# Two steps between norms or ternary weights and their transposes, and sums copied out of PSUM, in a four-layer network

## The chip, the core and the metric

The kernel runs on one core of one Trainium2 chip. The number that counts is the device time of one execution in microseconds (us). A core has four engines that compute and run side by side, each strictly in the order of its own queue: TensorE (PE in the profile; its weight loads, which overlap its matmuls, are PEld), VectorE (DVE), ScalarE (ACT) and GpSimd (POOL). They work on two memories on the chip, SBUF and PSUM; PE writes to PSUM alone. Three executions of the kernel before took 1842.01, 1845.6 and 1845.91 us, a median of 1845.6.

## The reference, cut to what matters

Four layers, each a cross-attention and then a feed-forward network, each added to `x` (2048 tokens of 256 numbers). The context has 1601 rows. The change lies in the feed-forward parts of the second and third layer (L1 and L2) and in what prepares their weights; the attention between them and after them is touched in passing.

```python
x = x + L0_xattn(layernorm(x), ctx)
x = x + L0_ffn(layernorm(x))
x = x + L1_xattn(layernorm(x), ctx, mask)
x = x + L1_ffn(layernorm(x))
x = x + L2_xattn(layernorm(x), ctx)
x = x + L2_ffn(layernorm(x))
x = x + L3_xattn(layernorm(x), ctx, mask)
x = x + L3_ffn(layernorm(x))

def L1_ffn(x):                      # 256 -> 1024 -> 256, rank 16 beside it
    h = bitlinear(x, w_fc) + gate * (x @ v.T @ fast_b.T @ u.T)
    r = maximum(h, 0)
    return bitlinear(r * r, w_proj) # weights rounded to -1, 0, 1 times a row's scale

def L2_ffn(x):                      # 256 -> 1024 -> 256
    h = gelu(ternary_linear(x, w_up))
    return ternary_linear(h, w_down)

def ternary_linear(x, w):           # weights -1, 0, 1 about half their mean size
    w_t = sign(w) * (abs(w) > 0.5 * mean(abs(w)))
    rms = sqrt(sum(x * x, -1)) / sqrt(x.shape[-1])
    return (x / (rms + 1e-8)) @ w_t.T
```

So the second `ternary_linear` of layer L2 divides each token's output by the root mean square of its 1024 hidden values, which is known only when all of them are.

## The kernel before, in words

**Tiles.** A partition is one of 128 rows (`P`). The tokens go in 4 chunks (`NCH`) of 512 (`CH`), each of 4 tiles of 128 tokens (`TPC`). `self.x` keeps all 16 tiles of the residual stream in SBUF. PSUM is shared out in three kinds of tiles: `psc`, 3 tiles of two banks each, for all products that are soon read; and one bank each of `pa` and `pm`, mostly for sums that stay for a while.

**Stages.** After layer 0's attention, `fast_layers` (L2503) runs seven stages: e0 (layer 0's feed-forward, to about 915 us of the profile), a1 (attention of layer 1, to 985), f1 (its feed-forward, to 1130), a2 (to 1335), f2 (to 1475), a3 (to 1735) and f3. Each stage is a loop of steps ("turns"). The order of PE is the order of the program, by hand: what the program issues first, PE does first. The orders of DVE, ACT and POOL are set when the kernel is built, close to the program's order.

**Work in the background.** While a stage's loop runs, two kinds of generators are advanced beside it. One prepares the weights of the next stage; it is opened and queued after 3/16 of the loop's turns. The other kind, `norm_into` (L1272), makes the normalized and transposed input of one chunk; `ahead(c)` at the start of chunk c completes the norm of chunk c and puts that of chunk c+1 at the front. After each turn `side` (L1258) advances the generator at the front by so many steps as the stage's rate says (2 in a1, f1, a2, f2), and a step ends at a `yield`. At the end of a loop `ready` runs what is left of the next stage's weights, and of its first norm, at once:

```python
def side(self, n=1):
    while n and self.bg:
        if next(self.bg[0], self) is self:
            self.bg.popleft()
        else:
            n -= 1

def finish(self, gen):
    while gen in self.bg:
        self.side()
    drain(gen)
```

`finish` advances by one step at a time. Where the norm at the front turns out to be at its end, `side` takes it away and runs one step of the generator behind it, the next weights.

**A norm.** `norm_into` has, for a chunk: statistics of the 4 tiles on DVE (two steps, L1278, L1279), the inverse root on POOL (one step, L1283 to L1293; in f2 with a root mean square too), four `xn` tiles on DVE (two steps, L1298), and then 8 transposes on PE into one `psc` tile (L1307) with copies out of it (one step): six steps. In f1 and f2 (`split`) the copies are `xh` on ACT (L1314, a cast to the format that PE takes at its full speed) and `xl` on DVE (L1315, what that cast left), alternating for two halves, each waiting for the one before.

**Feed-forward of layers 1 and 2, `fast_ffn` (f1 and f2).** A chunk has four turns. Turn n issues `up(n)`: 8 matmuls of 128x512 over `xh` and `xl` (L1708; in f1 two more, L1713, with `z`, a small product that `low_rank` makes at each chunk's start from `xh` and `xl`, L1691 to L1697); then `down(n - 2)`: 16 matmuls of 128x256 (L1749), which add to `accs`, the one `pa` and the one `pm` bank. Between them ACT, DVE and POOL turn the product into `hi` and `lo`: in f2 a gelu and a cast on ACT (L1718, L1719), `lo` and the square `sq` on DVE (L1720, L1722), and the sum of squares on POOL (L1728, L1730); in f1 ACT does L1734 and L1736, DVE the square L1735, POOL `lo` (L1737). So `down` of a chunk's last groups is issued after the first two `up` of the next chunk. `close(c)` follows the last `down` of a chunk: in f2 it sums the squares over the hidden values with matmuls by a column of ones (L1762), copies the four sums (L1767), makes the inverse root on POOL and DVE (`rms_inverse`, L157 to L160), and adds the four tiles to `x` (L1771) straight from the banks `pa` and `pm`. The next chunk's first `down` needs these banks again, and there is one of each.

**Ternary weights.** `ternary_transposed` (called by the weights generators of f1 and f2) makes the -1, 0, 1 tile `t` on DVE in six steps and then, in two steps, transposes it on PE (L1540) into a `psc` tile that ACT copies (L1541). In f1's weights, L1606 and L1616 belong to the small product that follows. L1350 to L1389 are in the weights of the attention a2, prepared during f1; L2120 is in those of a3, prepared during f2.

**Attention of layer 3, `fast3`.** Scores of a head group go through an exponential on ACT into `p` tiles (L2230), of which five are there; two are made for each group of 128 keys (L2223) and read by `values`. `verdict`, at the end of layer 0's attention, decides from the masks which branch is run; its tile `some` lies in the pool `small`.

Of the kernel before, what the change touches and what calls it, by code (L numbers as in the profile page):

```python
# [9 lines left out]
F32 = mybir.dt.float32  # L10
F32R = mybir.dt.float32r
BF16 = mybir.dt.bfloat16
AF = mybir.ActivationFunctionType
ALU = mybir.AluOpType
# [36 lines left out]
class Net:  # L51
# [1217 lines left out]
            self.side()  # L1269
        drain(gen)  # L1270

    def norm_into(self, pool, c, made, split=False, rms=False, bufs=2):  # L1272

        nc = self.nc
        st = self.small.tile([P, TPC, 6], F32, name="st")
        mv = self.small.tile([P, TPC, 2], F32, name="mv")
        for i in range(TPC):
            nc.vector.bn_stats(st[:, i, :], self.x[c * TPC + i])  # L1278
            nc.vector.bn_aggr(mv[:, i, :], st[:, i, :])  # L1279
            if i % 2:  # L1280
                yield
        rstd = self.small.tile([P, TPC], F32, name="rstd")
        nc.gpsimd.tensor_scalar_add(rstd, mv[:, :, 1], LN_EPS)  # L1283
        nc.gpsimd.tensor_tensor(rstd, rstd, self.mhalf, ALU.pow)
        if rms:

            r = self.small.tile([P, TPC], F32, name="rms")
            nc.gpsimd.tensor_tensor(r, mv[:, :, 1], self.phalf, ALU.pow)
            nc.gpsimd.tensor_tensor(r, r, rstd, ALU.mult)
            nc.gpsimd.tensor_scalar(r, r, 1e-8, None, ALU.add)  # L1290
            ri = self.small.tile([P, TPC], F32, name="rmsi")
            nc.vector.reciprocal(ri, r)
            nc.gpsimd.tensor_tensor(rstd, rstd, ri, ALU.mult)  # L1293
        yield
        xns = []
        for i in range(TPC):
            xn = pool.tile([P, D], F32, name="xn", bufs=4)
            nc.vector.tensor_scalar(  # L1298
                xn, self.x[c * TPC + i], mv[:, i, 0:1], rstd[:, i : i + 1], ALU.subtract, ALU.mult
            )  # L1300
            xns.append(xn)
            if i % 2:
                yield
        ps = self.psc()
        for kc in range(2):
            for i in range(TPC):
                nc.tensor.transpose(  # L1307
                    ps[:, kc, i * P : (i + 1) * P], xns[i][:, kc * P : (kc + 1) * P], self.ident
                )
        if split:  # L1310
            xh = pool.tile([P, 2, CH], F32R, name="xh", bufs=2)
            xl = pool.tile([P, 2, CH], F32R, name="xl", bufs=2)
            for kc in range(2):
                nc.scalar.copy(xh[:, kc, :], ps[:, kc, :])  # L1314
                nc.vector.tensor_tensor(xl[:, kc, :], ps[:, kc, :], xh[:, kc, :].bitcast(F32), ALU.subtract)  # L1315
            made[c] = xh, xl
        else:
            xnT = pool.tile([P, 2, CH], F32, name="xnT", bufs=bufs)
            nc.scalar.copy(xnT[:, 0, :], ps[:, 0, :])  # L1319
            nc.vector.tensor_copy(xnT[:, 1, :], ps[:, 1, :])  # L1320
            made[c] = xnT
        yield
# [199 lines left out]
    def ternary_transposed(self, rawp, w, half, nhalf, place):  # L1522


        nc = self.nc
        n, m = w.shape[1:]
        lo = rawp.tile([P, n, m], BF16, name="lo")
        t = rawp.tile([P, n, m], BF16, name="t")
        for h in range(2):
            ns, shape = slice(h * n // 2, (h + 1) * n // 2), [P, n // 2, m]  # L1530
            nc.vector.tensor_tensor(lo[:, ns, :], w[:, ns, :], nhalf[:, ns, :].to_broadcast(shape), ALU.is_lt)
            yield
            nc.vector.tensor_tensor(t[:, ns, :], w[:, ns, :], half[:, ns, :].to_broadcast(shape), ALU.is_gt)
            yield
            nc.vector.tensor_tensor(t[:, ns, :], t[:, ns, :], lo[:, ns, :], ALU.subtract)
            yield
        for out, blocks in place:
            ps = self.psc(BF16, 1024)
            for k, (o, i) in enumerate(blocks):
                nc.tensor.transpose(ps[:, 0, k * P : (k + 1) * P], t[:, o, i * P : (i + 1) * P], self.identb)  # L1540
            nc.scalar.copy(out, ps[:, 0, :])  # L1541
            yield
# [134 lines left out]
    def fast_ffn(self, st, tail):  # L1677
# [79 lines left out]
        def close(c):  # L1757
            if gelu:
                ps = self.psc()
                for i in range(TPC):  # L1760
                    for j in range(2):
                        nc.tensor.matmul(  # L1762
                            ps[:, 0, i : i + 1], lhsT=sqs[c][:, j, i * P : (i + 1) * P], rhs=self.ones[:, 0:1],
                            start=j == 0, stop=j == 1,
                        )
                ss = self.small.tile([P, TPC], F32, name="ss2")
                nc.vector.tensor_copy(ss, ps[:, 0, :TPC])  # L1767
                ri = self.rms_inverse(ss, NF * P)
                for i in range(TPC):
                    x = self.x[c * TPC + i]  # L1770
                    nc.vector.scalar_tensor_tensor(  # L1771
                        x, accs[c][i // 2][:, (i % 2) * D : (i % 2 + 1) * D], ri[:, i : i + 1], x, ALU.mult, ALU.add
                    )
            else:
                for b in range(2):
                    y = pool.tile([P, 2, D], F32, name="y")
                    nc.vector.tensor_tensor(
                        y, accs[c][b].rearrange("p (i d) -> p i d", i=2),
                        w["out"].unsqueeze(1).to_broadcast([P, 2, D]), ALU.mult,
                    )  # L1780
                    x = self.xc[c][:, 2 * b : 2 * b + 2, :]
                    nc.gpsimd.tensor_tensor(x, x, y, ALU.add)
# [388 lines left out]
    def fast3(self, st, tail):  # L2171
# [46 lines left out]
        def scores(u, kt):  # L2218
            g, q = u % G, queries[u][0]
            pair = [self.psc() for _ in range(2)]  # L2220
            for j in range(4):
                hs = slice(32 * j, 32 * j + 32)
                nc.tensor.matmul(  # L2223
                    pair[j // 2][:, j % 2, :], lhsT=w["kT"][hs, g, kt * P : (kt + 1) * P], rhs=q[hs, :],
                    start=True, stop=True,
                )
            weights[u, kt] = []
            for k in range(2):
                p = pool.tile([P, 2, CH], F32, name="p", bufs=5)
                nc.scalar.activation(p, pair[k], AF.Exp, scale=DH**-0.5)  # L2230
                weights[u, kt].append(p)

# [237 lines left out]
    def verdict(self):  # L2470

        nc = self.nc
        some = self.small.tile([P, KEPT], BF16, name="some", bufs=1)
        sums = self.const.tile([P, 4], F32, name="sums")
        said = self.const.tile([P, 1], mybir.dt.int32, name="said")
        nc.vector.tensor_reduce(sums[:, 0:1], self.fl, AX.XYZ, ALU.add)
        ps = self.pm()
        nc.tensor.matmul(ps[:, 0:1], lhsT=self.ones, rhs=sums[:, 0:1], start=True, stop=True)
        nc.vector.tensor_scalar(sums[:, 1:2], ps[:, 0:1], 0.0, None, ALU.is_equal)
        nc.vector.tensor_scalar(some, self.row0[0], 0.0, None, ALU.not_equal)  # L2480
        nc.vector.tensor_reduce(sums[:, 2:3], some, AX.X, ALU.max)
        nc.vector.tensor_tensor(sums[:, 3:4], sums[:, 1:2], sums[:, 2:3], ALU.mult)
        nc.vector.tensor_copy(said, sums[:, 3:4])
        return said
# [70 lines left out]
    def layers(self):  # L2555
        def weights1(w, r):
            away = w.tile([P, KEPT], F32, name="away1")
            self.nc.vector.tensor_scalar(away, self.row0[0], 0.0, NEG, ALU.is_equal, ALU.mult)
            return self.fast1_weights(w, r, "L1_xattn", NCTX - KEPT, KEPT, away=away)

        def weights2(w, r):
            return self.fast1_weights(w, r, "L2_xattn", 0, NCTX, biases=True)

        split = {"split": True}
        self.fast_layers([
            ("e0", "left", self.fast0_weights, {"bufs": NCH}, self.fast0, 64, 1, 15),
            ("a1", "right", weights1, {}, self.fast1, 16, 2),
            ("f1", "left", self.fast_ffn1_weights, split, self.fast_ffn, 16, 2),
            ("a2", "right", weights2, {}, self.fast1, 16, 2),
            ("f2", "left", self.fast_ffn2_weights, {"rms": True, **split}, self.fast_ffn, 16, 2),  # L2570
            ("a3", "right", self.fast3_weights, {}, self.fast3, 48, 1),
            ("f3", "left", self.fast_ffn3_weights, {}, self.fast_ffn3, 16, 2),
        ])
# [109 lines left out]
```

## Time and profile before

| what | value |
|---|---|
| runs of the kernel | 1842.01, 1845.6, 1845.91 us, median 1845.6 |
| the profiled execution | 1846.99 us |
| its span, first to last instruction | 1844.9 us |
| mean granted clock of TensorE | 0.956 of full |
| f1's transposes L1307 for chunks 1, 2, 3 start at | 1008.40, 1029.53, 1062.20 us |
| f2's sums L1762 start at | 1377.30, 1407.56, 1438.32, 1469.86 us |
| f2's transposes L1307 for chunks 1, 2, 3 start at | 1363.84, 1391.21, 1420.10 us |

The profile is of one execution. Its span is 2.1 us shorter than the time of that execution, and this execution was 1.4 us longer than the median. Times within it are in us from the first instruction. A line such as `PE pa L1749 <- DVE x L1771` says that matmuls of line 1749 into the tile `pa` stood waiting until instructions of line 1771 on DVE, which write `x`, were done. In a timeline a line gives the start, the duration, the engine, the source line, the operation, the tiles (out<-in), shapes, how many instructions are put together, and in brackets the idle time of the engine ahead of it with what ended that. In a table of stretches each engine has its busy time and its number of instructions, and PEclk is the clock that TensorE was granted, as a part of full speed; matmuls take longer when it is below 1.

### The profile page before, as it was taken

How to read it: one execution, taken by the hardware profiler on the slowest of the kernel's cores; microseconds unless marked ns; L12 is line 12 of the kernel's file. 1: busy time of each engine (PE TensorE's matmuls, PEld its weight loads, DVE VectorE, ACT ScalarE, POOL GpSimd, SP SyncE). 2: the span in 40 equal slices, each digit the busy share in tenths (PEclk: the TensorE clock that was granted, in tenths of full speed). 3: DMA queues.
4: the chain of work that ended last, by engine and by line, in shares of the span. 5: the costliest groups of instructions: out<-in, count | busy, mean ns of one | idle time of the engine just before them, and what ended most of it. 6: DMA issues, size and time to landing. Idle time of an engine off the chain costs nothing. (4 is left out here: it accounts for less than half of the span.)

```text
span 1844.9 us, 20264 instructions
## 1 busy us (share of the span) xinstructions
PE 1676.9 (91%) x7939; PEld 892.9 (48%) x7939; DVE 969.7 (53%) x1697; ACT 683.1 (37%) x968; POOL 621.0 (34%) x480
## 2 busy tenths in 40 slices
PE   5669999999999997995999889999987899999999
PEld 3223334334333333542466756677666633333687
DVE  4446665665666553155385323434467767666200
ACT  3564443443443341121334341222243244545421
POOL 4135765765565664006302441000045411000010
PEclk9989999999999998797998899999987989999999
DMA  8750000000000001222410000000010030000151
GB/s 206 124 90 1 1 1 1 1 1 1 0 1 1 1 1 66 74 109 79 173 48 1 1 1 15 9 1 1 23 30 1 16 131 7 1 4 1 60 175 48
DMA packets 40282, 69.23 MB, mean 38 GB/s; under 512 B 5085, under 2 KB 28014, under 8 KB 40174
## 3 DMA queue, kind: packets, MB, share of 16 engines
q1 hardware_dynamic: 28240, 33.97, 5.7%
q0 software_dynamic: 5664, 15.42, 4.8%
q10 hardware_dynamic: 6270, 18.42, 2.5%
q8 instruction: 66, 1.08, 0.2%
q14 instruction: 42, 0.34, 0.1%
HBM read 62.22 MB, written 18.89 MB: 44 GB/s over the span
## 5 line engine op out<-in xcount | busy, mean ns | idle before, releaser
L465 POOL TENSOR_TENSOR sp<-sp,p 128x1024 f32<-128x1024 f32 (+1 forms) x128 | 306.6, 2395 | 189.9 <-ACT p L450 181.4
L450 ACT ACTIVATE p<-psc 128x1024 f32<-128x1024 f32 (+1 forms) x208 | 212.7, 1023 | 266.4 <-PE psc L446 262.3
L368 DVE TENSOR_REDUCE mp<-psc 128x2 f32<-128x1024 f32 x192 | 232.1, 1218 | 138.3 <-PE psc L364 132.3
L443 PE MATMUL psc<-qT,kT 64*128 64x512 f32 (+1 forms) x832 | 224.3, 616 | 12.8 <-DVE mp L368 12.8
L474 PE MATMUL pa<-p,v 128*64 128x512 f32 (+1 forms) x832 | 203.5, 607 | 0.0
L2207 DVE TENSOR_REDUCE mst<-psc 128x2 bf16<-128x800 f32 x128 | 124.6, 994 | 59.4 <-PE psc L2203 58.3
L1850 PE MATMUL psc<-ew,xnT 128*128 128x512 f32 x256 | 128.4, 659 | 5.9 <-PEq L1954 4.1
L1495 PE MATMUL pa<-v,pT 128*128 128x256 f32 (+2 forms) x544 | 126.0, 382 | 1.8 <-ACT pT L1485 1.2
L443 PEld LDWEIGHTS psc<-qT,kT 64*128 64x128 f32 (+1 forms) x832 | 69.0, 182 | 115.4 <-issue 53.6
L1444 PE MATMUL psc<-kT,xnT 128*128 128x512 f32 (+2 forms) x320 | 119.3, 512 | 2.7 <-ACT xnT L1319 1.4
L2230 ACT ACTIVATE p<-psc 128x1024 f32<-128x1024 f32 x96 | 93.1, 1021 | 62.7 <-PE psc L2223 61.1
L1283 POOL TENSOR_SCALAR rstd<-mv 128x4 f32<-128x4 f32 x28 | 7.3, 259 | 309.4 <-DVE mv L1279 304.4
L1495 PEld LDWEIGHTS pa<-v,pT 128*128 128x128 f32 (+2 forms) x544 | 99.6, 190 | 19.5 <-issue 4.3
L474 PEld LDWEIGHTS pa<-p,v 128*64 128x64 f32 (+1 forms) x832 | 50.0, 136 | 89.5 <-issue 86.7
L500 DVE RECIPROCAL t<-t 128x128 f32<-128x128 f32 x64 | 54.2, 909 | 68.0 <-ACT t L495 68.0
L1850 PEld LDWEIGHTS psc<-ew,xnT 128*128 128x128 f32 x256 | 52.7, 211 | 69.6 <-issue 65.2
L364 PE MATMUL psc<-kb,qb 64*128 64x512 bf16 x384 | 74.8, 381 | 9.6 <-ACT p L450 9.5
L1856 ACT COPY y<-psc 128x1024 f32<-128x1024 f32 x32 | 32.4, 1012 | 136.0 <-PE psc L1850 130.9
L1485 ACT COPY pT<-psc 128x512 f32<-128x512 f32 (+1 forms) x48 | 26.4, 550 | 152.2 <-PE psc L1476 152.2
L446 PE MATMUL psc<-shift,onerow 64*128 64x512 bf16 (+1 forms) x416 | 79.7, 376 | 1.6 <-ACT shift L395 1.6
L1444 PEld LDWEIGHTS psc<-kT,xnT 128*128 128x128 f32 x320 | 55.2, 190 | 50.8 <-issue 41.0
L364 PEld LDWEIGHTS <-qb 64*128 64x128 bf16 x384 | 27.0, 94 | 93.5 <-issue 91.8
(378 smaller groups left out, 2806.6 us busy)
## 6 DMA issues: line engine op xcount, KB each, us to landing
table<-y ACTq DMA_DIRECT2D x32, 512.0 KB, 2.6
w<-in_L_ffn_w_dram SPq DMA_DIRECT2D x16, 1024.0 KB, 5.5
w_look<-in_mask_BxSxS_ik_dram POOLq DMA_DIRECT2D x16, 400.2 KB, 4.6
w_look<-in_mask_1x1xSxS_ik_dram POOLq DMA_DIRECT2D x16, 400.2 KB, 4.5
x<-in_x_dram SPq DMA_DIRECT2D x4, 512.0 KB, 10.2
ew<-in_L_ffn_experts_dram SPq DMA_DIRECT2D x2, 1024.0 KB
out_dram<-y SPq DMA_DIRECT2D x8, 256.0 KB, 5.5
raw<-in_ctx_dram ACTq DMA_DIRECT2D x3, 512.0 KB, 10.1
```

What stands on the lines that cost most here:

```text
L364: nc.tensor.matmul(ps[:, j, :wd], lhsT=qb[hs, i * P : (i + 1) * P], rhs=kb[hs, hp, k0 : k0 + wd], start=True, stop=True,)
L368: nc.vector.tensor_reduce(mp[:, :, i, n], ps, AX.X, ALU.max)
L443: nc.tensor.matmul(sc[:r, j, :], lhsT=kT[hs, hp, ks], rhs=q[hs, :], start=True, stop=False)
L446: nc.tensor.matmul(sc[:r, j, :], lhsT=self.onerow[hs, :r], rhs=shifts[u][hs, :], start=False, stop=True)
L450: nc.scalar.activation(p[:r], sc[:r], AF.Exp, scale=DH**-0.5)
L465: eng.tensor_tensor(old[:r], old[:r], p[:r], ALU.add)
L474: nc.tensor.matmul(acc[j * DH : (j + 1) * DH, :], lhsT=v[:r, kt, (2 * hp + j) * DH : (2 * hp + j + 1) * DH], rhs=p[:r, j, :], start=kt == ...
L1444: nc.tensor.matmul(ps[:, b // CH, :wd], lhsT=xnT[:, kc, i * P : (i + 1) * P], rhs=kT[:, kc, g0 + b : g0 + b + wd], start=kc == 0, stop=kc ...
L1495: nc.tensor.matmul(acc[:, :D], lhsT=pT[:r, kt, :], rhs=v[:r, kt, :], start=kt == 0, stop=kt == nkt - 1)
L1850: nc.tensor.matmul(ps[:, q % 2, :], lhsT=norms[t // TPC][:, kc, (t % TPC) * P : (t % TPC + 1) * P], rhs=w["e"][kc][:, 2 * q : 2 * q + 2, : ...
L2207: nc.vector.tensor_reduce(top[:, 2 * k : 2 * k + 2, DH], ps[:, :, :KEPT], AX.X, ALU.max)
L2230: nc.scalar.activation(p, pair[k], AF.Exp, scale=DH**-0.5)
```

## The change

Five edits in one diff:

- `norm_into` gets a parameter `wait`: so many yields, with no work, between the last `xn` and the transposes. `split`, the options of the norms of f1 and f2, sets it to 2: eight steps in place of six. The other norms keep 0.
- `ternary_transposed` yields twice between its last DVE step and its first transposes, for f1's and f2's weights.
- `close` of f2 copies `pa` and `pm` with ACT into two SBUF tiles `y` (two buffers), right behind the L1762 matmuls in the program, and the updates of `x` read `y`.
- `p` in `fast3` has four buffers in place of five.
- `some` in `verdict` moves from the pool `small` to the pool `xnp`.

```diff
@@ -1269,7 +1269,7 @@
             self.side()
         drain(gen)
 
-    def norm_into(self, pool, c, made, split=False, rms=False, bufs=2):
+    def norm_into(self, pool, c, made, split=False, rms=False, bufs=2, wait=0):
 
         nc = self.nc
         st = self.small.tile([P, TPC, 6], F32, name="st")
@@ -1301,6 +1301,8 @@
             xns.append(xn)
             if i % 2:
                 yield
+        for _ in range(wait):
+            yield
         ps = self.psc()
         for kc in range(2):
             for i in range(TPC):
@@ -1534,6 +1536,8 @@
             yield
             nc.vector.tensor_tensor(t[:, ns, :], t[:, ns, :], lo[:, ns, :], ALU.subtract)
             yield
+        yield
+        yield
         for out, blocks in place:
             ps = self.psc(BF16, 1024)
             for k, (o, i) in enumerate(blocks):
@@ -1763,14 +1767,16 @@
                             ps[:, 0, i : i + 1], lhsT=sqs[c][:, j, i * P : (i + 1) * P], rhs=self.ones[:, 0:1],
                             start=j == 0, stop=j == 1,
                         )
+                ys = []
+                for b in range(2):
+                    ys.append(pool.tile([P, 2, D], F32, name="y", bufs=2))
+                    nc.scalar.copy(ys[-1].rearrange("p i d -> p (i d)"), accs[c][b])
                 ss = self.small.tile([P, TPC], F32, name="ss2")
                 nc.vector.tensor_copy(ss, ps[:, 0, :TPC])
                 ri = self.rms_inverse(ss, NF * P)
                 for i in range(TPC):
                     x = self.x[c * TPC + i]
-                    nc.vector.scalar_tensor_tensor(
-                        x, accs[c][i // 2][:, (i % 2) * D : (i % 2 + 1) * D], ri[:, i : i + 1], x, ALU.mult, ALU.add
-                    )
+                    nc.vector.scalar_tensor_tensor(x, ys[i // 2][:, i % 2, :], ri[:, i : i + 1], x, ALU.mult, ALU.add)
             else:
                 for b in range(2):
                     y = pool.tile([P, 2, D], F32, name="y")
@@ -2226,7 +2232,7 @@
                 )
             weights[u, kt] = []
             for k in range(2):
-                p = pool.tile([P, 2, CH], F32, name="p", bufs=5)
+                p = pool.tile([P, 2, CH], F32, name="p", bufs=4)
                 nc.scalar.activation(p, pair[k], AF.Exp, scale=DH**-0.5)
                 weights[u, kt].append(p)
 
@@ -2470,7 +2476,7 @@
     def verdict(self):
 
         nc = self.nc
-        some = self.small.tile([P, KEPT], BF16, name="some", bufs=1)
+        some = self.xnp.tile([P, KEPT], BF16, name="some", bufs=1)
         sums = self.const.tile([P, 4], F32, name="sums")
         said = self.const.tile([P, 1], mybir.dt.int32, name="said")
         nc.vector.tensor_reduce(sums[:, 0:1], self.fl, AX.XYZ, ALU.add)
@@ -2561,7 +2567,7 @@
         def weights2(w, r):
             return self.fast1_weights(w, r, "L2_xattn", 0, NCTX, biases=True)
 
-        split = {"split": True}
+        split = {"split": True, "wait": 2}
         self.fast_layers([
             ("e0", "left", self.fast0_weights, {"bufs": NCH}, self.fast0, 64, 1, 15),
             ("a1", "right", weights1, {}, self.fast1, 16, 2),
```

## The prediction

> **What bounds the kernel now.** I read the page first (busy time, clock slices), then the waits of PE over the layers that the change can reach, then the stretches of layer 2's feed-forward (f2), then its engines side by side in the timeline. The page makes TensorE the bound:
>
> ```profile
> PE 1676.9 (91%) x7939; PEld 892.9 (48%) x7939; DVE 969.7 (53%) x1697; ACT 683.1 (37%) x968; POOL 621.0 (34%) x480
> ```
>
> All other engines have room, so only what makes PE wait, or lowers its clock, is worth time. PE's waits from 905 us (the end of layer 0) to the end; columns are total, times, longest:
>
> ```profile
> PE pa L1749 <- DVE x L1771: 11.2, 2, 6.3
> PE psc L1540 <- DVE t L1535: 6.2, 2, 4.7
> ...
> PE psc L1362 <- DVE xl L1315: 4.2, 1, 4.2
> ...
> PE psc L1307 <- DVE xn L1298: 3.6, 2, 2.0
> ...
> PE psc L1389 <- DVE xl L1315: 2.5, 1, 2.5
> ```
>
> These five, 27.7 us, are what the diff touches: the first is f2's banks, the last three are norms, the second is a ternary transpose. They come to 1.5% of the span: little is to be had. The same f2 cut at the starts of L1762 (one sits at the end of each chunk), and two short stretches of it (columns: us, then busy time of each engine, granted clock of PE, DMA):
>
> ```profile
> 1377.30:1407.56 30.26, 21.94 (x127) 19.46 (x126) 23.95 (x35) 10.12 (x13) 18.09 (x15) 0.83 0.00 1
> 1407.56:1438.32 30.76, 24.27 (x139) 21.21 (x138) 19.00 (x32) 11.20 (x15) 13.53 (x12) 0.83 0.00 1
> 1438.32:1469.86 31.54, 27.57 (x154) 20.20 (x153) 25.50 (x45) 7.78 (x9) 18.64 (x16) 1.00 0.00 1
> ...
> 1382.00:1389.00 7.00, 1.59 (x6) 1.40 (x7) 2.85 (x9) 1.20 (x2) 4.24 (x7) 0.66 0.00 0
> 1412.00:1423.00 11.00, 5.16 (x21) 4.58 (x22) 8.02 (x14) 1.46 (x2) 5.52 (x8) 0.64 0.00 0
> ```
>
> The first two chunk periods lose PE time (clock 0.83), the third does not (1.00): a wait costs twice, once as idle time and once as a low clock behind it. PE's work in one chunk at full clock, from its rows: 4 up groups (8.0) + 4 down groups at 2.07 (8.3) + transposes 1.03 + L1762 1.84 = 19.2. Period one: 30.26 - 19.2 - waits (6.32 + 1.99) leaves 2.8 for the low clock; period two: 30.76 - 19.2 - (4.89 + 1.59) leaves 5.1.
>
> **The edits, one by one.**
>
> *Sums copied out (L1771).* Now PE's next down group waits until the four x updates have read the banks, and those wait for a chain on POOL. DVE and POOL around it:
>
> ```profile
> 1380.20 3.26 POOL L1728 TENSOR_TENSOR sqs<-sq 128x1024 f32<-128x1024 f32 x1 [3.44 <-DVE sq L1722]
> 1383.43 1.01 POOL L157 TENSOR_TENSOR rms<-ss,phalf 128x4 f32<-128x4 f32 x1
> 1384.42 1.00 POOL L1288 TENSOR_TENSOR rms<-mv,phalf 128x4 f32<-128x4 f32 x1
> 1385.50 0.20 POOL L158 TENSOR_SCALAR rms<-rms 128x4 f32<-128x4 f32 x1
> ```
> ```profile
> 1385.73 0.18 DVE L160 RECIPROCAL rmsi<-rms 128x4 f32<-128x4 f32 x1 [4.40 <-POOL rms L158]
> ...
> 1386.42 0.85 DVE L1771 SCALAR_TENSOR_TENSOR x<-pa,rmsi,x 128x256 f32<-128x256 f32 x2
> 1387.18 0.87 DVE L1771 SCALAR_TENSOR_TENSOR x<-pm,rmsi,x 128x256 f32<-128x256 f32 x2
> 1387.97 0.72 DVE L1298 TENSOR_SCALAR xn<-x,mv,rstd 128x256 f32<-128x256 f32 x2
> 1388.61 1.22 DVE L1720 TENSOR_TENSOR lo<-h,hi 128x1024 fp32r<-128x1024 f32 x1
> 1389.75 1.22 DVE L1722 TENSOR_TENSOR sq<-h 128x1024 f32<-128x1024 f32 x1
> 1390.88 2.75 DVE L1298 TENSOR_SCALAR xn<-x,mv,rstd 128x256 f32<-128x256 f32 x2
> ```
>
> The change adds two ACT copies of 128x512 out of PSUM. L480 is that copy: 0.586 us each, 8 in all, 4.7 us of ACT. The last down group ends at 1377.30, and PE comes back to a bank after L1762 (1.84) and one up group (1.93), at 1381.07. ACT idles from 1377.7 to 1381.1, so 2 x 0.586 fit: cost nothing; without that cover up to 1.2 per chunk. The x update from SBUF costs what it did from PSUM (L1976 481 ns, L1771 470). So the waits 6.32 and 4.89 at L1749 go.
>
> What is late next: the same chain, one place further. The x updates still stand ahead of the next chunk's last xn in DVE's queue, with lo, sq and a POOL sum that stretches xn to 2.75. The transposes L1307 need all four xn. PE, no longer held, does down, up, down (2.07 + 2.0 + 2.07) from 1381.07 and stands at L1307 at about 1387.2, 1388 with something lost. The last xn ends at 1393.5 in the trace's order; the earliest it can be is 1388.2 (rstd is ready at 1386.8, four xn at 0.36). So the new wait there lies between 0 and 5.5; I take 4.3, nearest to the order in the trace.
>
> *Norms leave two steps (f1, f2).* The generator now has eight steps, as many as a chunk has turns, so L1307 goes from behind the third up group of a chunk to right ahead of the next chunk's first matmul that reads xh and xl. Nothing is between them. The copies are serial, xh 0.585 on ACT and xl 0.69 on DVE, twice: 2.55, with semaphores 2.65 (1394.49 to 1398.4 in the trace with other work between). Before, two groups of PE hid this. From the end of the transposes to the last xl the trace has 3.83, 10.0, 7.3 (f1) and 5.45, 4.0, 2.68 (f2): with busy queues that is the other end. I take 2.65, because an idle PE sends nothing new into those queues.
>
> *f2 summed.* Where the norm is finished right ahead of its use, the loop also runs one step of the next weights in the gap; I count one like L2120 (four transposes, 0.60), so 2.05 of each 2.65 shows. Into chunk 1 (no x update is near): -2.05. Into chunk 2: before 6.32 + 1.99 + 2.8 = 11.1; after 4.3 + 2.05 + 1.0 of low clock (half of the 1.9 that a down group lost, 3.96 against 2.07) = 7.35; +3.75. Into chunk 3: before 4.89 + 1.59 + 5.1 = 11.6; after 7.35; +4.25. Into layer 3's attention, where two steps of weights have moved behind the loop: -0.6 (one such step). Sum +5.3. If the xn wait is nil and the clock stays full: +16; with the row 5.45 in place of 2.65 at the three boundaries: -3.
>
> *f1 summed.* Here the norm's slot of psc, held until xl is done, stops the next weights' L1362 for 4.18 and L1389 for 2.54, with a clock of 0.63 in 1037 to 1047 (about 2 us). With the transposes later, these weight steps find the slot free: +8.7. Three boundaries now show 2.65 = 8.0, less the weights steps that run there (L1350, L1362 with L1367, and L1378: 1.75, 2.4 and 0.5 of PE work) = 4.65. That would be +5.4. With the rows 3.83, 10.0 and 7.3, less 1 us of cover each, less 4.65: a loss of 13.5, so -4.8. Between ends that far apart I take the middle, +0.3: the chain's row is long where ACT has an activation and a cast ahead of it (L1734 1.27, L1736 1.05), and these are still ahead of it.
>
> *Ternary transposes leave two steps.* In f1's weights only the first place moves, behind one attention item; then L1606's cast follows another 1.0 us cast: -0.6. In f2's, the 4.7 wait at L1540 is a chain of six DVE compares which runs after the loop, where the generator is drained with no PE work between two steps: a bare yield separates nothing there. 0, bounded by +-1.6, the smaller wait of that row. *p with 4 buffers, `some` in another pool:* a score group is issued behind the values that read the p it overwrites, so 0; up to -0.8 (the longest L2203<-p) if not.
>
> Sum: 5.3 + 0.3 - 0.6 = **5.0 faster**. The profiled execution took 1846.99 (span 1844.9 and 2.1 around it), so 1842.0 there. The median of the runs is 1845.6, 1.4 lower: 1840.6.
>
> **Two rules weighed.** DVE's sq took 3.42 at 1374.43 (1.22 alone), until POOL's L1730 ended at 1376.77: the two exclude each other here. The Trainium skill ("SBUF — State Buffer", "SBUF: two separate sides") says why: a DVE operation with two SBUF inputs and a GpSimd one that reads SBUF cannot hold the shared ports together, and the later waits to the end. That speaks against this change: the x update had one SBUF input (x), and gets two (y, x). By the trace POOL has 0.2 us operations at that time, so little; by the rule, if one POOL sum of 2.44 comes first at each of three chunks, 7 us go and the sum is -2.
> The clock was 0.66 in 1382 to 1389, behind a 6.3 wait. "TensorE: Matmul & The Clock Gate" (Part 1) halves the clock after an idle window of about 3.4 us, and in Part 4 says that transposes don't count as busy. Then 4.3 + 1.03 + 2.65 is one window and the low clock stays as long as now: 2.8 and 5.1 in place of 1.0 each, a sum of about -1.
>
> **Rivals.**
> A, full release: xn comes before PE does, the chunk takes 19.2 + 2.65 = 21.9, twice 30.5 becomes 22: +17, less 3 for the other seams, and 4 more or less in f1: 10 to 18 faster, about 1832. For: ACT and POOL are idle half of the time. Against: rstd is not ready before 1386.8, and DVE is busy 23.95 of 30.26.
> B, the exposed chain: xh and xl beside their use at six boundaries at the length of the rows, 33.2 in all, less 1 us of cover each, is 27; against it stand 11.2 + 4.2 + 2.5 + 3.6 = 21.5 of waits that go and 4.65 of hidden weights. If the xn wait of 4.3 comes back twice it is 27 + 8.6 - 26 = 9 to 10 slower, about 1855. It decides from 3.9 us of exposed chain at a boundary on: (26 - 8.6) / 6, and the 1 us of cover.
> C, it only moves: L1307<-xn and the boundary take exactly what L1749<-x had (19.2 + 11 stays the period): 1844 to 1847. Also so if the bare yields separate nothing.
>
> **Numbers.** Forecast (1836 to 1844): 0.41. A: 0.20. C: 0.14. B (1847 and up): 0.25. A measurement of this kernel can tell some 0.2%, 3.7 us, from no change. The forecast lies partly within it (0.10 of its 0.41): faster 0.31 + 0.20 = 0.51; same 0.10 + 0.14 = 0.24; slower 0.25. The range leaves out the ends of A and B: 1831 to 1852.
>
> **What would show it.** Right: L1749<-x gone, L1307<-xn at 3 to 5 twice, new waits of 2 to 3 of L1708 or L1691 for xh or xl at six places, starts of L1762 some 26 to 28 apart, clock above 0.83, L1362 and L1389 no longer behind xl, the 4.7 at L1540 still there. Wrong: L1762 22 apart (A); boundary waits of 4 to 7 (B); waits behind POOL sums in the x update (the port rule); longer waits of layer 3 for p.

## The result, and the profile after

The changed kernel took 1850.6 us (median of 9 runs), the kernel before 1844.8 (9 runs beside it): a ratio of 1.0031, 95% interval 1.0018 to 1.0043. It is slower; the forecast was 5 us faster. Measured again later beside other kernels the ratio was 1.0009 (0.9996 to 1.0022), which alone would not tell it from no change. The single runs of one kernel lie some 8 us apart, and the profiles show where much of that comes from: in layer 0's attention every kernel here issues the same work, and its last update of x ended between 723.8 and 730.5 us. So the stages behind it are compared one by one below. Where the code and the granted clock are the same, they agree to 0.1 or 0.2 us from profile to profile. Where the clock differs they don't: f1 with the same code took 138.2 or 137.1, and f2 with the code of before took 124.8 to 127.6 (its last part alone 31.54 at a clock of 1.00 and 34.44 at 0.90). A difference below that in one profile is not a gain or a loss by itself.

Page 1 of the changed kernel's profile, and the first lines of PE's waits from 905 us on (total, times, longest):

```profile
PE 1681.6 (91%) x7939; PEld 893.4 (48%) x7939; DVE 967.5 (52%) x1697; ACT 686.7 (37%) x976; POOL 620.8 (34%) x480
```
```profile
PE psc L1695 <- ACT xh L1316: 11.4, 4, 5.4
PE psc L1309 <- DVE xn L1298: 8.5, 4, 2.3
PE psc L1544 <- DVE t L1537: 6.0, 2, 4.5
```

(Lines behind 1300 have moved: L1307 is now L1309, L1314 L1316, L1540 L1544, L1691 L1695, L1749 L1753.) The wait at the banks (11.2) is gone, and so are those of the next weights behind xl (4.2 and 2.5). In their place PE waits for xh at the low-rank product of f1, and for xn. All waits of over 0.35 us from 956 to 1520 us come to some 52 us both before and after: the idle time has moved.

f2 in the same four parts as before, cut where the closing matmuls start (L1766 now):

```profile
1347.14:1384.40 37.26, 32.93 (x159) 27.39 (x160) 18.72 (x30) 15.85 (x18) 17.59 (x19) 0.86 0.13 36
1384.40:1411.91 27.51, 23.15 (x126) 19.75 (x125) 20.85 (x34) 11.02 (x15) 17.18 (x15) 0.81 0.00 1
1411.91:1440.16 28.25, 23.97 (x134) 20.56 (x133) 17.49 (x30) 12.17 (x17) 13.10 (x11) 0.82 0.00 1
1440.16:1471.32 31.16, 28.49 (x159) 21.00 (x158) 24.50 (x46) 7.52 (x11) 18.73 (x17) 1.00 0.00 1
```

The second and third are 2.8 and 2.5 shorter than before, the fourth 0.4; the first is 4.9 longer (32.34 before). f1, from its first low-rank product to the next attention's transposes, before and then after:

```profile
990.07:1128.25 138.18, 123.93 (x592) 95.05 (x593) 49.75 (x90) 51.00 (x75) 51.41 (x30) 0.93 0.00 1
```
```profile
989.86:1130.91 141.05, 122.59 (x593) 93.09 (x593) 54.04 (x90) 51.14 (x75) 51.38 (x30) 0.95 0.00 1
```

PE is less busy in a longer stage: f1 lost 2.9 us by waiting. From the end of layer 0's attention on, the profile of the change is 4.2 us longer: 2.9 in f1, 0.9 in a1 (where f1's ternary weights are made), 0.9 in a3, and 0.8 in e0, where the code is the same and the clock was 0.845 in place of 0.857; a2 and f2 are 0.5 and 0.7 shorter.

### The profile page after: what moved, and what is told of

Its sections match the earlier page's. It is cut to its first block, busy times and chain, and to the rows that moved or that the text cites. A ratio compares the mean times of both kernels' runs of the same rounds, so it can differ in the third digit from the quotient of the medians.

```text
span 1847.2 us, 20271 instructions
## 1 busy us (share of the span) xinstructions
PE 1681.6 (91%) x7939; PEld 893.4 (48%) x7939; DVE 967.5 (52%) x1697; ACT 686.7 (37%) x976; POOL 620.8 (34%) x480
## 4 chain that ended last, share of the span: by engine, by line
PE 41%; DVE 6%; ACT 3%; issue 1%; POOL 1%; DMA 1%; SPq 0%; DVEq 0%; ACTq 0%; POOLq 0%
PE pa L1497 7%; PE psc L1446 6%; PE psc L2229 3%; PE psc L2406 3%; PE psc L1712 3%; PE psc L1856 2%; PE pa L2252 2%; PE pm L2424 1%; PE pa L2424 1%; PE psc L1478 1%; PE pm L2193 1%; PE psc L2209 1%; PE pa L1753 1%; PE pm L1753 1%; PE pm L2242 1%
## 5 line engine op out<-in xcount | busy, mean ns | idle before, releaser
L368 DVE TENSOR_REDUCE mp<-psc 128x2 f32<-128x1024 f32 x192 | 232.2, 1218 | 138.1 <-PE psc L364 132.0
```

The source lines that it names most:

```text
L368: nc.vector.tensor_reduce(mp[:, :, i, n], ps, AX.X, ALU.max)
```

## The experiments

All ratios are to the kernel before, run beside on the same chip. f1 and f2 are the lengths of the two stages in the profile, cut as above (f2: the sum of its four parts).

| kernel | ratio (95% interval) | f1 us | f2 us |
|---|---|---|---|
| before | 1 | 138.2 | 124.9 |
| the change | 1.0031 (1.0018 to 1.0043) | 141.1 | 124.2 |
| the change again | 1.0009 (0.9996 to 1.0022) | 141.6 | 122.7 |
| f1's steps alone | 1.0014 (1.0003 to 1.0025) | 141.3 | 124.8 |
| f2's steps alone | 1.0013 (1.0003 to 1.0023) | 138.2 | 127.0 |
| copies alone | 1.0016 (1.0007 to 1.0025) | 138.1 | 128.4 |
| ternary yields alone | 1.0001 (0.9990 to 1.0011) | 137.1 | 124.8 |
| f2's steps and copies | 0.9969 (0.9957 to 0.9981) | 137.1 | 124.4 |
| p and `some` alone | 0.9993 (0.9982 to 1.0005) | 138.2 | 124.9 |
| the change without f1's steps | 0.9984 (0.9971 to 0.9997) | 137.2 | 124.3 |
| copies, earlier root in f2 | 0.9953 (0.9939 to 0.9966) | 138.1 | 120.0 |
| earlier root, no copies | 0.9966 (0.9954 to 0.9977) | 138.2 | 121.4 |
| copies, earlier root, first sum on DVE | 0.9942 (0.9929 to 0.9955) | 138.2 | 113.3 |
| f1's steps, lo on DVE | 0.9976 (0.9964 to 0.9988) | 134.2 | 127.6 |
| before, lo on DVE | 0.9949 (0.9930 to 0.9969) | 127.6 | 125.3 |
| the change, lo on DVE | 0.9978 (0.9965 to 0.9990) | 134.1 | 124.2 |
| first sum and lo on DVE, copies, root | 0.9897 (0.9877 to 0.9917) | 127.5 | 112.0 |
| the same with f1's steps | 0.9913 (0.9895 to 0.9932) | 134.2 | 114.1 |

**Each part alone.** Theory F1: f1's two steps are the loss. Rival F2: f2 or the copies are.

```diff
-            ("f1", "left", self.fast_ffn1_weights, split, self.fast_ffn, 16, 2),
+            ("f1", "left", self.fast_ffn1_weights, {"wait": 2, **split}, self.fast_ffn, 16, 2),
```

That is f1's steps alone; f2's alone set the same in f2's line. The copies and the ternary yields are the change's own lines, each without the rest.

> Only the norms of f1 leave two steps; all else is the kernel before. Theory F1 (the change's loss comes from f1, where PE stands at the low-rank product behind xh for about 5 us at the starts of chunks 2 and 3): those two waits of 4 to 6 us are there, the waits of 4.2 and 2.5 of the next weights behind xl are gone, and the kernel is 2 to 5 us slower, a ratio of 1.001 to 1.003. Theory F2 (the loss comes from f2 or from the copies): within 1.5 us of before.

> Only the norms of f2 leave two steps, without the copies. Theory F1: the waits of the down groups for the x updates (6.3 and 4.9) stay, they now also cover the late xn, so no wait for xn is left, but each of three boundaries shows 2 to 3 us for xh and xl; slower by 2 to 6 us. Theory F2: the same waits, and slower by 5 us or more, since all of the loss is here or in the copies.

> Only the copies out of the banks (with the four p buffers and the moved tile that make room for them); the norms keep their place. Theory F1: the waits at the banks go, and what is late next is xn: the transposes stand where they stood, PE comes to them 4 us earlier and waits 8 to 10 us for xn at chunks 2 and 3; the time is within 3 us of before. Theory F2, if the copies are the loss: slower by 5 us or more. If the copies gave what the prediction hoped: faster by 5 us or more.

> Only the two yields in the ternary weights. Both theories: the first place of f1's weights moves behind one attention item, two waits of 1.1 become 1.5 to 1.6, 0.5 to 1 us slower; f2's weights keep their wait of 4.5 to 4.7. A ratio of 0.9995 to 1.001. A third theory, that these yields are what costs: slower by 4 us or more.

f1's steps alone cost what the whole change costs in f1 (141.3 against 138.2). f2's steps alone lose 2.1 in f2 and the copies alone 3.5: both theories had a share. These two sizes are rough, since the clock alone moves f2 that far (1.3 of the 3.5 is in the last part, at 0.95 in place of 1.00); by the ratios each is 2 to 3 us slower. Without the copies f2's steps left 4.2 and 4.1 us at the banks, not the 6.3 and 4.9 expected, and up to 2.9 behind xl. The copies by themselves take the wait from the banks to xn, since the transposes still stand two turns ahead. PE's first wait in that kernel:

```profile
PE psc L1307 <- DVE xn L1298: 18.0, 6, 5.5
```

That is the 11.2 and 3.6 of before, and 3 more. The ternary yields are worth nothing that can be measured.

**Together.** In the first of these the yields in the ternary weights and f1's steps are out, in the second only the room is made.

> The change without its part in f1 and without the two yields in the ternary weights: f2's copies and f2's two steps together, with the room they need. Each alone was 2.4 to 3 us slower than before. Theory M (the two belong together: the copies take the wait from the banks to xn, the two steps hide a part of that): waits for xn of 4 to 4.5 at chunks 2 and 3, no wait at the banks, and within 2 us of before. Theory S (the losses add up, whatever they hide of each other): 5 to 6 us slower.

> Only the four buffers for p and the tile in another pool, the two edits that make room. Theory M: no wait changes, within 1.5 us of before. A rival, that the lost buffer delays layer 3's attention: the waits of its scores for p, 4.5 in 12 before, grow to 7 or more and the kernel is 2 to 4 us slower.

f2 takes 124.4 where the parts alone took 127.0 and 128.4: they belong together (theory M), and come out 0.5 ahead of before, which is within what the clock does. By the ratio of 0.9969 the kernel is 5.7 us faster, past the 2 us of theory M; its stages give about 0.3. I go by the stages; where the rest comes from is not shown. p and `some` cost nothing.

> The changed kernel once more, beside the next two on one chip, since its time (5.8 us over before) and the sum of its parts do not agree: f1's two steps alone measured 2.6 slower, f2's part 5.7 faster, the ternary yields nothing. Stages of the profiles, from the end of layer 0's attention on, give 4.3 slower in all. Theory M (parts as the stages show them): 2 to 6 us slower than before, a ratio of 1.001 to 1.003. Rival I (an interaction of f1's and f2's parts): 5 to 8 us slower, and 8 or more over the kernel without f1's two steps.

> The change with only f1's two steps undone. Theory M: f1's part costs about 3 us by the stages, 4 at most, so this kernel lies 3 to 5 us under the changed one and within 2 us of before; the waits for xh of 4.9 and 5.4 in f1 are gone. Rival I: 8 or more under the changed one, and 3 to 6 faster than before.

On one chip, undoing f1's steps took the median from 1850.9 to 1844.3, the ratio from 1.0009 to 0.9984 (4.6 us) and f1 from 141.6 to 137.2 (4.4, of which 1.0 is the clock). By ratio and stage that is theory M, though the medians lie 6.6 apart and the changed kernel was only 1.7 us over before by its ratio (theory M had 2 to 6); the 8 of rival I are not reached. f1 is the main part of the loss.

**What makes f1's chain long.** The changed kernel's timeline at the start of f1's chunk 3 (start, duration, idle time and its releaser in brackets):

```profile
1068.18 2.34 POOL L1741 TENSOR_TENSOR lo<-h,hi 128x1024 fp32r<-128x1024 f32 x1
1068.90 2.71 DVE L1739 TENSOR_TENSOR h<-h 128x1024 f32<-128x1024 f32 x1 [2.12 <-ACT h L1738]
1071.64 1.04 ACT L1740 CAST hi<-h 128x1024 fp32r<-128x1024 f32 x1 [2.78 <-DVE h L1739]
1072.59 0.58 ACT L1316 CAST xh<-psc 128x512 fp32r<-128x512 f32 x1
...
1073.22 0.79 PE L1695 MATMUL psc<-xh,vhT 128*128 128x512 f32 x1 [5.37 <-ACT xh L1316]
```

The transposes were done at 1067.4, but xh stands on ACT behind hi of the last up group, hi waits for the square on DVE, and the square (1.21 alone) takes 2.71: it ends 1.1 after POOL's lo, as if it had begun only then. The test puts lo on DVE, with f1's steps alone otherwise:

```diff
-                nc.gpsimd.tensor_tensor(lo, h, hi.bitcast(F32), ALU.subtract)
+                nc.vector.tensor_tensor(lo, h, hi.bitcast(F32), ALU.subtract)
```

> f1's two steps alone, with f1's lo made by DVE in place of POOL, so that no large POOL operation runs beside DVE there. Theory L (a good part of the exposed chain is DVE waiting for POOL: four xn took 3.40 in place of 1.45, the square 2.71 in place of 1.21, both beside lo on POOL): with 2.35 of POOL gone and 1.2 of DVE added, these rows fall to 1.5 and 1.2, and PE's waits for xh at the starts of chunks 2 and 3 fall from 4.9 and 5.4 to 3 to 4.2. Rival (the chain is long because the cast hi and the square stand ahead of xh in any case): the waits stay at 4.5 to 5.5. The time may go either way, since DVE has 1.2 more per group.

The same place in that kernel:

```profile
1063.32 1.22 DVE L1737 TENSOR_TENSOR h<-h 128x1024 f32<-128x1024 f32 x1
...
1064.57 1.04 ACT L1738 CAST hi<-h 128x1024 fp32r<-128x1024 f32 x1 [1.29 <-DVE h L1737]
1065.52 0.58 ACT L1316 CAST xh<-psc 128x512 fp32r<-128x512 f32 x1
...
1066.15 0.50 PE L1693 MATMUL psc<-xh,vhT 128*128 128x512 f32 x1 [1.47 <-ACT xh L1316]
```

The square is at 1.22 and the wait fell from 5.37 to 1.47 (at chunk 2 from 4.88 to 1.81), below what theory L expected. Only a part of that is instructions that took longer beside POOL: 1.5 in the square at chunk 3, and 2.0 in an xn at chunk 2 (2.43 in place of 0.40). The chain also began late in the changed kernel, as DVE stood behind POOL's update of x, and that behind another lo:

```profile
1064.74 0.75 DVE L1278 BATCH_NORM_STATS2 st<-x 128x6 f32<-128x256 f32 x2 [2.64 <-POOL x L1788]
```

The edit took that wait away too. But which is to blame, the steps or DVE and POOL? That was open, and the next two told:

> The kernel before with f1's lo made by DVE in place of POOL, without any leaving of steps. With f1's two steps the same edit cut f1's stage (first low-rank product to the transposes of the next attention) from 141.3 to 134.2, where the kernel before has 138.2. Theory L (the two steps are harmless in themselves, what costs is that DVE and POOL shut each other out in the chain that they lay bare): without the steps the stage is at 134 to 137, and the steps then cost or gain less than 1.5. Theory W (the two steps cost 3 in any case): the stage is at 131 or less.

> The changed kernel with f1's lo made by DVE. Theory L: the changed kernel's loss is gone: f1's stage at 134 to 135 in place of 141, the whole 5 to 9 us under the changed kernel and 2 to 6 under the kernel before. Theory W: the same stage, but then the kernel before with this edit is 3 faster than this one in f1.

Theory L falls. Without f1's steps the same edit gives 127.6: the steps cost 6.6 there, more than the 2.9 of the change and twice the 3 of theory W. With them PE still waits some 6 us for xh and xl at the chunks' starts.

Why 10.6 us shorter? The waits of 4.2 and 2.5 behind xl in the kernel before are gone with the edit, and so is much low clock (f1's clock went from 0.93 to 0.97). What had made those waits was not DVE and POOL slowing each other's instructions, but the order of POOL's queue. At the first, xl stood on DVE behind xn, xn behind POOL's inverse root, and that behind lo:

```profile
1035.20 2.35 POOL L1737 TENSOR_TENSOR lo<-h,hi 128x1024 fp32r<-128x1024 f32 x1 [3.13 <-issue]
1037.83 1.04 POOL L1284 TENSOR_TENSOR rstd<-rstd,mhalf 128x4 f32<-128x4 f32 x1
```
```profile
1038.90 1.06 DVE L1298 TENSOR_SCALAR xn<-x,mv,rstd 128x256 f32<-128x256 f32 x3 [2.63 <-POOL rstd L1284]
1039.88 0.68 DVE L1315 TENSOR_TENSOR xl<-psc,xh 128x512 fp32r<-128x512 f32 x1
```

At the second it was POOL's update of x that came behind lo, and the statistics and the square on DVE behind that (hi, xh and xl follow the square):

```profile
1061.11 2.38 POOL L1737 TENSOR_TENSOR lo<-h,hi 128x1024 fp32r<-128x1024 f32 x1
1063.45 1.29 POOL L1782 TENSOR_TENSOR x<-x,y 128x512 f32<-128x512 f32 x1
```
```profile
1064.78 0.76 DVE L1278 BATCH_NORM_STATS2 st<-x 128x6 f32<-128x256 f32 x2 [2.62 <-POOL x L1782]
1065.44 1.21 DVE L1735 TENSOR_TENSOR h<-h 128x1024 f32<-128x1024 f32 x1
```

Over the whole of f1, DVE waited 12.8 us for POOL's small results before and 1.9 with lo on DVE. Lengthened instructions cannot be the reason: POOL lengthened DVE's squares in f1 by 1.0 us in all before, and its squares and lo by 3.0 with the edit. (In the changed kernel it was 5.3: the steps put xn and squares beside lo.) PE waited for lo itself in neither kernel. No run changes lo's place in POOL's queue alone, so this is read from the traces. The steps too removed the waits behind xl, and lost more than that at the chunks' starts. Where lo is off POOL, there is nothing left for them to gain.

**What holds f2.** The norm's inverse root is issued one step earlier, and the transposes leave one step, so that they keep their old place.

```diff
-            if i % 2:
+            if i % 2 and not (early and i == 1):
                 yield
```

> f2's copies; f2's norms do both pairs of statistics in one step and then leave one step, so that their transposes stand where they stood before the change, but the inverse root is issued one step earlier, ahead of the chunk's closing and of the sums of squares on POOL. Theory P (what holds PE is the chain on POOL behind which xn comes): no wait at the banks, none for xn, none of over 1 us for xh or xl; the starts of the closing matmuls 22 to 25 us apart, clock of 1 in chunks 1 to 3, and 8 to 16 us faster than before. A rival, Q (DVE or ACT is the next bound, POOL's chain hides nothing): other waits of 4 us and more take their place and the time stays within 3 us of before.

> The same earlier inverse root in f2, transposes in their old place, but without the copies: the x updates still hold the banks. Theory P: the waits for xn (2.0 and 1.6) go, those at the banks stay near 6 and 5 less what POOL gains by doing one root earlier (1 us each), so 2 to 5 us faster than before, and the copies are worth the rest, 6 to 10 us. Rival Q: no difference to before, and none to the kernel with the copies.

With it the copies are worth 1.5 in f2 (120.0 against 121.4; the clock alone can do that), not 6 to 10. Neither theory holds fully: no xn is late, but without the copies the waits at the banks are 6.4 and 6.8, and with them two waits of PE of 4.6 and 5.8 at L1710 remain. The cause of the first in the timeline of the kernel with the copies:

```profile
1382.91 3.32 POOL L1730 TENSOR_TENSOR sqs<-sq 128x1024 f32<-128x1024 f32 x1 [3.78 <-DVE sq L1724]
...
1386.19 1.02 POOL L157 TENSOR_TENSOR rms<-ss,phalf 128x4 f32<-128x4 f32 x1
...
1388.51 0.18 DVE L160 RECIPROCAL rmsi<-rms 128x4 f32<-128x4 f32 x1 [4.47 <-POOL rms L158]
...
1393.05 0.68 DVE L1317 TENSOR_TENSOR xl<-psc,xh 128x512 fp32r<-128x512 f32 x1
...
1395.32 0.80 PE L1710 MATMUL psc<-xh,wuT 128*128 128x512 f32 x1 [4.57 <-ACT h L1720]
```

DVE stands 4.47 at the head of its queue behind a root that POOL does only after a sum of squares. The first of a chunk's sums went to DVE:

```diff
-                    nc.gpsimd.tensor_tensor(sqs[c], old, sq, ALU.add)
+                    nc.vector.tensor_tensor(sqs[c], old, sq, ALU.add)
```

> The kernel with the copies and the earlier inverse root in f2, and with the first of a chunk's three sums of squares added by DVE in place of POOL. In the kernel without this edit DVE stood 4.5 us behind rmsi, whose root on POOL came after a sum of 3.3, and xl with all behind it waited; PE then waited 4.6 and 5.8. Theory P (that sum is what holds the root): DVE's idle time before rmsi falls from 4.5 to 1 to 2, PE's waits of 4.6 and 5.8 to under 3 each, the starts of the closing matmuls come 22 to 25 us apart, and the kernel is 2 to 7 us faster than without the edit, 10 to 14 faster than before. Rival (DVE's added 1.2 eats it): waits move by less than 1 us and so does the time.

DVE's wait for the root fell to 2.40 (theory P had 1 to 2), no wait of PE there is over 2.9, the closing matmuls start 25.2 and 23.8 apart, and f2 takes 113.3: theory P. Both edits together:

> f2 with the copies, the earlier inverse root and the first sum on DVE (113.3 in f2 in place of 124.9), and f1's lo on DVE, f1's norms as before. If the two add up: 11 in f2 and what the edit gives in f1 (1 to 5), 12 to 16 us faster than before.

> The same with f1's two steps. Theory L: within 1.5 us of the one without them in f1's stage; Theory W: 3 slower.

The gains add: 1827.2 us, 0.9897 (0.9877 to 0.9917), the fastest kernel here. f1's steps on top cost 6.7 in f1 once more (127.5 to 134.2).

## Why the prediction was wrong

- *The copies.* Right as far as they go: no wait at the banks, the copies take 0.58 each at 1384.70 in idle ACT time, and the x updates are not slower (four in 1.66). The wait that takes the place, forecast at 4.3 twice, was 2.27 + 2.02 and 2.19 + 2.01.
- *f1, +0.3 forecast, -2.9 measured (-3.4 in the second profile).* This step failed: the price of the bare chain from transposes to copies. "I take 2.65, because an idle PE sends nothing new into those queues": what holds xh is in the queues already (a cast behind a square, that behind statistics, and these behind POOL). At the three boundaries PE stood 0.9, 4.9 and 5.4 us, 11.1 in all, where 2.65 each, less the weights steps, gave 3.3, and the rows 3.83, 10.0 and 7.3 gave 13.5. The chain came out near the end that the rows gave, and the middle of the two ends was a choice without a row. The waits behind xl went as forecast (6.7).
- *f2, +5.3 forecast (5.95 within the stage and -0.6 behind it), +0.7 measured in the stage (2.2 in the second profile).* Terms were mis-sized here, by the clock above all. Into chunk 1 I forecast -2.05 of bare chain; the idle time was 2.4, but the whole part became 4.9 longer, since the stretch from the first up product to the closing matmuls went from 8.83 to 12.70:

```profile
1368.47:1377.30 8.83, 8.31 (x51) 6.81 (x50) 8.25 (x7) 6.33 (x7) 6.91 (x5) 1.00 0.00 1
```
```profile
1371.70:1384.40 12.70, 10.95 (x48) 9.07 (x49) 5.83 (x8) 4.33 (x5) 7.04 (x4) 0.73 0.00 0
```

 The first line is before, the second after: granted clock 1.00, then 0.73. Into chunks 2 and 3 I took 2.05 of bare chain and 1.0 for the low clock; with 19.2 of work and 4.3 and 4.2 of waits, 27.51 and 28.25 leave 4.0 and 4.8 for the low clock, and hardly any other wait is there: the bare chain did not show. So +3.75 and +4.25 became +2.75 and +2.5.
- *Seams and ternary weights.* -0.6 into layer 3's attention came out so: 38.16 became 38.77 us from the last closing matmuls to the transposes of that stage's second chunk (all of a3: 0.9 longer). The first ternary places wait 0.9 longer in f1's weights; alone, 1.0001.
- *The two rules.* The clock rule was the better guide: by it (the Trainium skill, "TensorE: Matmul & The Clock Gate", Part 1 and Part 4) the sum was 1 us slower. The clock was in fact as low as before (0.81 and 0.82, before 0.83 and 0.83). The port rule (the Trainium skill, "SBUF — State Buffer", "SBUF: two separate sides") was weighed at the x update, where POOL had no operation of over 0.6 us, and four updates took 1.66 to 1.74, before 1.63 to 1.66. It bore on f1, where the squares and xn stand beside POOL's lo: 2.71 and 1.22 for the same square are this trace's numbers for it, and 2.43 and 0.40 for an xn. It also came true at the x update, but in the kernels with the first sum on DVE: there one of the four updates stood beside POOL's next sum and took 2.62 in place of 0.47, at two chunks.
- *Rivals.* B was nearest: exposed chains of about 5 at two boundaries, above the 3.9 from which it decides. It took six alike, and the other four were smaller: f1's into chunk 1 showed 0.9, f2's into chunk 1 2.4, and f2's other two, behind the wait for xn, none.

## What to carry to other kernels

A producer that is moved next to its consumer lays bare not its own copies but everything that its queue holds ahead of them; take the measured time from producer to last copy, not the sum of the copies. Before an order is changed to hide a wait, follow its chain through the other engines' queues to the large operation that stands ahead: taking lo out of POOL's queue gave 10.6 us in f1, where the reordering lost 2.9. A small operation at the head of an in-order queue, here a 128x4 reciprocal behind POOL's root, can hold PE two engines further on.

## What the runs showed of the hardware

In f2's chunk 1, idle times of 0.7 and 1.8 us on PE, one on each side of the first matmul behind 1.0 us of transposes, were followed by a stretch of low clock (0.73 over 12.70 us, where it had been 1.00 over 8.83): 3.9 longer, with 1.8 of it idle. DVE's square of 128x1024 took 1.22 alone. All five squares of the changed kernel's f1 that ran while POOL was in a subtraction ended 1.1 after it, whenever they had begun; the longest took 2.71. The subtraction took 2.34 to 2.43 on POOL and mostly 1.23 on DVE (1.9 to 2.0 three times). Of the two ways in which POOL held DVE in f1 of the kernel before, waits for POOL's small results (12.8 us) weighed more than instructions that POOL lengthened (1.0 us).
